# A delta-rule layer's decay gate: softplus as one activation from PSUM, its four activations queued together

## Chip, core and metric

One Trainium2 chip, one of its NeuronCores. The metric is the device time of one launch in microseconds (us). A core has five engines that run their own instruction queues in order: TensorE (PE; its weight loads are shown as PEld), VectorE (DVE), ScalarE (ACT), GpSimd (POOL) and SyncE (SP), which here only starts DMA transfers. Engines wait for each other by semaphores.

## The reference

Six residual steps on x of 1024 tokens by 256 columns: feed-forward, sliding-window attention, feed-forward (twice, with different weights), a gated delta-rule layer with 16 heads of 128, and a last feed-forward. The change is in the delta-rule layer. Cut to what matters:

```python
q = short_conv(hidden @ Wq, conv_q)      # k and v alike: 4 taps, then silu
g = (hidden @ Wfa @ Wfb).reshape(B, T, H, DV) + dt_bias
g = exp(-softplus(g) * exp(A_log))       # the decay gate, per token, head and column
q, k = l2norm(q) * DK ** -0.5, l2norm(k)
def step(S, (qt, kt, vt, gt, bt)):       # over the tokens
    S = S * gt[..., None]
    delta = (vt - einsum("bhk,bhkv->bhv", kt, S)) * bt[..., None]
    S = S + kt[..., None] * delta[:, :, None, :]
    return S, einsum("bhk,bhkv->bhv", qt, S)
```

So for every token, head and column a gate exp(-softplus(z) * a) is computed from z = g + dt_bias, with a one positive number per head.

## The kernel before

**The stages.** Feed-forward and attention take the first 590 us or so; then `delta_rule` runs to the end, with the last feed-forward (`network`) woven into its last turns. The change touches `delta_rule` alone.

**The tiling.** Tokens are cut into 8 tiles of 128, heads into 4 groups of 4. A *pair* is two neighbouring token tiles of one head group; there are 4 x 4 = 16 pairs. Columns of a head lie on the 128 partitions, and a pair's tile is [128, 2 token tiles, 4 heads, 128 tokens], that is 1024 numbers per partition.

**The steps of one pair,** each a Python generator that yields between its steps:

- `prepare`: `convolved` for k and then q. Per head it projects into a PSUM tile `ps` (L641), multiplies the first tap on ScalarE (L653) and adds three taps on VectorE (L655); then Silu over the tile (L660). The squares go to ScalarE (`sq`, L674) and their sums over the partitions to TensorE (`pss`, L678), which VectorE moves out (`ss`, L681). Then the gate: a matmul per head into `pg` (L700), the chain of activations below, and last `pq` (L732), `qk` (L736) and the products `kq` = k times gate on VectorE (L741) and q times gate on POOL (L742).
- `triangle`: seven levels, 1 to 64. Each has matmuls `pm` of k against `kq` (L791; the last is L803), then multiplies `kq` (VectorE, L813) and k (POOL, L819) by the running gate `d`, and puts masked results into `ml` and `qk` (VectorE, L855 and L856). `ml` goes to DRAM as `dm` (L844).
- `solve`: reads blocks of `dm` back (`xb`), scales them into `nb` (L905) and inverts 16 x 16 blocks by small VectorE operations, to `zb` (L943) and on POOL `ztb` (L945); eight transfers (L953, L954) spread them.
- `join`: VectorE steps `four` (L969), `zm` (L972), `four` (L974), `add` (L977), then ScalarE and DMAs to the tiles `z` and `zt`.
- `invert`: matmuls from `pmz` (L1016) on that finish the inverse. `values`, `gates`, `advance` and `emit` make v, the output gate, the recurrent state and the output (`pw`, `pn`, `pso`, `px`).

**The gate's chain before the change** (in `prepare`): per head an Identity from PSUM to SBUF with the bias column dt_bias (L708). Then, over the whole tile, softplus(z) = max(z, 0) + ln(1 + exp(-|z|)): Abs (L716), Exp (L717), Ln (L718) on ScalarE, max and add on VectorE (L720). Last an Exp per head with scale -a (L722) into `ge`. `p["d"]` is `ge`, so the triangle uses it too.

**What sets the order.** The main loop (L1224 on) works on four pairs at once in turn i: `prepare` of pair i+2, `triangle` of pair i+1, `solve`, `join`, `invert`, `values`, `gates` of pair i, and `advance` and `emit` of pair i-1. `weave` sorts the steps: a lane (begin, end, n, steps) has n steps spread evenly between begin and end of the turn; the lane of `prepare` is (0.0, 1.0, 21). On top of that the tile layer schedules: it may move an instruction within its engine's queue by its own estimate of times, so the order of a queue isn't that of the text. `tc.issue_after(ins)` keeps what it encloses behind a given instruction.

**PSUM.** The pool `pj` has three buffers, which `ps`, `pss`, `pg`, `pq`, `ptv`, `pgo` and the last feed-forward's tiles take in turn. An activation function that isn't in ScalarE's loaded table set needs a table load first, an instruction of its own in ScalarE's queue (ACT_TABLE_LOAD in the profile, with the line of the activation that needs it).

Of the kernel before, what the change touches and what calls it, by code (L numbers as in the profile page):

```python
# [1 line left out]

# [8 lines left out]
F32 = mybir.dt.float32  # L11
I32 = mybir.dt.int32
BF16 = mybir.dt.bfloat16
AF = mybir.ActivationFunctionType
ALU = mybir.AluOpType
# [3 lines left out]
P = 128  # L19
# [5 lines left out]
HD = 128  # L25
# [11 lines left out]
HG = 4  # L37
# [441 lines left out]
def key_weights(nc, pool, a, g):  # L479

    cs = slice(g * HG * HD, (g + 1) * HG * HD)
    w = {}
    for nm, src in (("k", "dWk"), ("q", "dWq")):
        w[nm] = pool.tile([P, KC, HG * HD], F32, name=f"w{nm}")
        nc.sync.dma_start(out=w[nm], in_=a[src][:, cs].rearrange("(c p) i -> p c i", p=P))
    w["fb"] = pool.tile([P, HG * HD], F32, name="wfb")
    nc.sync.dma_start(out=w["fb"], in_=a["dWfb"][:, cs])
    return w


def value_weights(nc, pool, a, g):

    cs = slice(g * HG * HD, (g + 1) * HG * HD)
    w = {}
    w["v"] = pool.tile([P, KC, HG * HD], F32, name="wv")
    nc.sync.dma_start(out=w["v"], in_=a["dWv"][:, cs].rearrange("(c p) i -> p c i", p=P))
    w["gb"] = pool.tile([P, HG * HD], F32, name="wgb")
    nc.sync.dma_start(out=w["gb"], in_=a["dWgb"][:, cs])
    w["o"] = pool.tile([P, HG, D], F32, name="wdo")
    nc.sync.dma_start(out=w["o"], in_=a["dWo"][cs, :].rearrange("(h p) d -> p h d", p=P))  # L500
    return w


def delta_rule(tc, a, x, xnT, pp, bc, kon, ones, kdw, first, store, xo):
# [24 lines left out]
    nc = tc.nc  # L529
# [6 lines left out]
    def all_heads(ap):  # L536

        return ap.unsqueeze(1).to_broadcast([P, 2 * HG, ap.shape[1]])

    with ExitStack() as ctx:  # L540
# [3 lines left out]
        pj = ctx.enter_context(tc.tile_pool(name="dpj", reuse_waits="tile", bufs=3, space=PSUM))  # L544
# [12 lines left out]
        faT = cst.tile([P, T], F32, name="faT")  # L557
        gaT = cst.tile([P, T], F32, name="gaT")
        for w, dst in ((wfa, faT), (wga, gaT)):
            for hf in range(2):  # L560
                ps = pj.tile([P, 512], F32, name="ps", tag="pj")
                for c in range(KC):
                    nc.tensor.matmul(
                        ps,
                        lhsT=w[:, c, :],
                        rhs=xnT[:, c, PAD + hf * 512 : PAD + (hf + 1) * 512],
                        start=(c == 0),
                        stop=(c == KC - 1),
# [4 lines left out]
        for n in range(NT):  # L573
            for c in range(KC):
                nc.tensor.matmul(
                    pb[:, n, :],
                    lhsT=xnT[:, c, PAD + n * P : PAD + (n + 1) * P],
                    rhs=wb[:, c, :],
                    start=(c == 0),
                    stop=(c == KC - 1),  # L580
# [3 lines left out]
        nea = cst.tile([P, NH], F32, name="nea")  # L584
# [79 lines left out]
        def prepare(us):  # L664

            g, pr, w = us[0]["g"], us[0]["n"] // 2, us[0]["w"]
            t0 = pr * 2 * P

            ss = small.tile([P, 2, 2, HG], F32, name="ss")
            for i, (nm, ccol) in enumerate((("k", C_CK), ("q", C_CQ))):  # L670
                yield from convolved(us, nm, ccol)
                sq = pre.tile([P, 2, HG, P], F32, name="sq", tag="tmp")
                for c in range(2):
                    nc.scalar.square(sq[:, c], us[0]["p"][nm][:, c])  # L674
                yield
                pss = pj.tile([P, 2, HG], F32, name="pss", tag="pj")
                for c, h, half in parts:
                    nc.tensor.matmul(  # L678
                        pss[half, c, h : h + 1], lhsT=sq[:, c, h, half], rhs=ones, start=True, stop=True
                    )  # L680
                nc.vector.tensor_scalar_add(ss[:, i], pss, 1e-6)  # L681
                yield
            cf = small.tile([P, 2, HG], F32, name="cf", bufs=3)
            nc.vector.reciprocal(cf, ss[:, 0])
            nc.vector.tensor_mul(cf, cf, beta[:, 2 * pr : 2 * pr + 2, g * HG : (g + 1) * HG])
            cfd = us[0]["cfd"] = dram.tile([2, HG, P], F32, name="cfd", bufs=4)
            nc.sync.dma_start(out=cfd.rearrange("c h r -> r c h"), in_=cf)
            kn = small.tile([P, 2, HG], F32, name="kn", bufs=4)
            nc.gpsimd.tensor_tensor(kn, ss[:, 0], plus.rearrange("p (c h) -> p c h", c=2), ALU.pow)

            qe = small.tile([P, 2, HG], F32, name="qe", bufs=5)
            nc.vector.tensor_scalar_mul(qe, ss[:, 1], 1e-6 * HD)


            y = pre.tile([P, 2, HG, P], F32, name="gy", tag="tmp")
            e = pre.tile([P, 2, HG, P], F32, name="ge")
            for h in range(HG):
                if h % 2 == 0:
                    pg = pj.tile([P, 2, 2 * P], F32, name="pg", tag="pj")
                nc.tensor.matmul(  # L700
                    pg[:, h % 2, :],
                    lhsT=w["fb"][:, h * HD : (h + 1) * HD],
                    rhs=faT[:, t0 : t0 + 2 * P],
                    start=True,
                    stop=True,
                )
                hd = C_DTB + g * HG + h
                nc.scalar.activation(  # L708
                    y[:, :, h, :],
                    pg[:, h % 2, :].rearrange("p (c t) -> p c t", t=P),  # L710
                    AF.Identity,
                    bias=pp[:, hd : hd + 1],
                )
                yield
            ef, yf = (t.rearrange("p c h t -> p (c h t)") for t in (e, y))
            nc.scalar.activation(ef, yf, AF.Abs)  # L716
            nc.scalar.activation(ef, ef, AF.Exp, scale=-1.0)  # L717
            nc.scalar.activation(ef, ef, AF.Ln, bias=1.0)  # L718
            yield
            nc.vector.scalar_tensor_tensor(yf, yf, 0.0, ef, ALU.max, ALU.add)  # L720
            for h in range(HG):
                nc.scalar.activation(  # L722
                    e[:, :, h, :], y[:, :, h, :], AF.Exp, scale=nea[:, g * HG + h : g * HG + h + 1]
                )
            yield
            for c, u in enumerate(us):
                u.update(kn=kn[:, c], qe=qe[:, c])
            p = us[0]["p"]
            k, q = p["k"], p["q"]
            pq = pj.tile([P, 2, HG, 64], F32, name="pq", tag="pj")  # L730
            for c, h, half in parts:
                nc.tensor.matmul(  # L732
                    pq[half, c, h], lhsT=k[:, c, h, half], rhs=q[:, c, h, half], start=True, stop=True
                )
            qk = p["qk"] = lev.tile([P, 2 * HG, 64], F32, name="qk", bufs=2)
            nc.vector.tensor_mul(  # L736
                qk, pq.rearrange("p c h t -> p (c h) t"), all_heads(kon[:, K_I : K_I + 64])
            )
            kq = p["kq"] = lev.tile([P, 2, 2, HG, P], F32, name="kq", bufs=3)
            p["d"] = e  # L740
            nc.vector.tensor_mul(kq[:, 0], k, e)  # L741
            nc.gpsimd.tensor_mul(kq[:, 1], q, e)  # L742
            yield
# [474 lines left out]
        for i in range(NG * NT // 2):  # L1218
            g, pr = divmod(i, NT // 2)
            p = dict(turn=turns[i % 2])  # L1220
# [3 lines left out]
        for i in range(-2, len(pairs) + 2):  # L1224
            ahead, mid, now, past = at(i + 2), at(i + 1), at(i), at(i - 1)
            lanes = []
            if ahead:
                g = ahead[0]["g"]
                if g and ahead[0]["n"] == 0:
                    keyw = key_weights(nc, kdw, a, g)  # L1230
                for u in ahead:
                    u["w"].update(keyw)
            if now:
                g = now[0]["g"]
                if g and now[0]["n"] == 0:
                    valw = value_weights(nc, kdw, a, g)
                for u in now:
                    u["w"].update(valw)
            if past:
                lanes.append((0.0, 0.35, 12, chain(advance(past[0]), emit(past[0]), advance(past[1]), emit(past[1]))))  # L1240
            if now:
                lanes.append((0.05, 0.2, 14, solve(now, vbs[i % 2])))
                lanes.append((0.2, 0.35, 6, join(now)))
                lanes.append((0.6, 0.95, 5, invert(now)))
                lanes.append((0.1, 0.65, 7, values(now)))
            if mid:
                lanes.append((0.1, 0.7, 9, triangle(mid)))
            if ahead:
                lanes.append((0.0, 1.0, 21, prepare(ahead)))
            if now:  # L1250
                lanes.append((0.5, 1.0, 2, gates(now)))
            qr = i - len(pairs) + 2
            if qr == 0:
                last_weights()
            if qr >= 0:
                lanes.append((0.2, 0.8, 10, network(qr)))
            weave(*lanes)
# [103 lines left out]
```

## Time and profile before

| | |
|---|---|
| median of three runs | 1770.35 us (1765.06 to 1772.35) |
| span of the profiled execution, first to last instruction | 1763.3 us |
| PE busy | 1409.2 us (80%) |
| VectorE busy | 1236.7 us (70%) |
| ScalarE busy | 847.7 us (48%) |
| POOL busy | 548.2 us (31%) |
| mean granted TensorE clock | 0.886 |
| first and last start of the gate's last Exp (L722) | 645.4 and 1601.7 us |
| ScalarE table loads in the gate | 48 of 1283 ns (L717, L718, L722, 16 each) |
| VectorE step of softplus (L720) | 16 of 1226 ns |
| `kq` on VectorE (L741), one of 16 | 1221 to 3369 ns, median 2252 |

The span is that of one profiled execution; the runs' times come from executions of their own, and the median is 7 us above the span. Busy shares are means over stages with different limits: what a step costs is read from the stage in which it stands, by the engine that waits there and what ends the wait. An operation is named by what it writes and reads ("ge<-gy,nea"), with the line of the kernel.

### The profile page before, as it was taken

The numbers are of one execution on the slowest core, as the hardware profiler recorded it, in microseconds if no ns is written. First come the engines' busy times: TensorE is split into PE (matmuls) and PEld (weight loads), VectorE is DVE, ScalarE is ACT, GpSimd is POOL, SyncE is SP. The second block draws the span as 40 slices with busy tenths as digits, with TensorE's granted clock in tenths as the row PEclk, the third lists the DMA queues.
The fourth block names the chain that finished last, engine by engine and source line by source line (L and its number), as shares of the span: only waits on it lengthen the run. The fifth ranks groups of instructions, "written<-read, shape, count | busy, mean of one in ns | idle before, by whom it ended". The sixth has DMA issues, their size and how long they took to land.

```text
span 1763.3 us, 30888 instructions
## 1 busy us (share of the span) xinstructions
PE 1409.2 (80%) x11697; PEld 1035.2 (59%) x11712; DVE 1236.7 (70%) x2565; ACT 847.7 (48%) x2242; POOL 548.2 (31%) x486
## 2 busy tenths in 40 slices
PE   7986777867899866678867977977887878788996
PEld 3535453635454554466756756765766766676775
DVE  2367889797832247778877787787788688698721
ACT  2227171726222344356646655656645646655431
POOL 0021323231000024244354254353254353354310
PEclk9998898889899967689988888988988988899998
DMA  6020000000200200221121221122221121122100
GB/s 233 1 45 9 5 22 7 5 27 8 89 18 0 48 1 15 35 41 36 34 37 26 46 45 30 32 31 44 41 52 22 35 42 34 34 47 45 30 21 12
DMA packets 185957, 61.09 MB, mean 35 GB/s; under 512 B 148560, under 2 KB 178064, under 8 KB 185552
## 3 DMA queue, kind: packets, MB, share of 16 engines
q1 hardware_dynamic: 185808, 59.11, 15.6%
q8 instruction: 93, 1.52, 0.4%
q14 instruction: 56, 0.46, 0.1%
HBM read 39.64 MB, written 12.75 MB: 30 GB/s over the span
## 4 chain that ended last, share of the span: by engine, by line
PE 34%; DVE 15%; issue 6%; ACT 6%; DMA 5%; POOL 4%; SPq 3%; DVEq 0%; POOLq 0%; ACTq 0%
PE ps L641 4%; PE pm L791 3%; PE po L160 3%; PE pg L135 2%; PE pu L135 2%; DVE k L655 2%; DVE kq L813 2%; PE px L1123 2%; DMA z<-z 2%; PE pss L678 2%; PE pw L1074 1%; PE pgu L1175 1%; PE pgo L762 1%; POOL k L819 1%; DMA dm<-ml 1%
## 5 line engine op out<-in xcount | busy, mean ns | idle before, releaser
L791 PE MATMUL pm<-kq,k 128*64 128x64 f32 x3072 | 140.7, 252 | 133.3 <-DVE kq L741 65.9
L791 PEld LDWEIGHTS pm<-kq,k 128*64 128x64 f32 x3072 | 124.1, 163 | 160.2 <-issue 97.5
L819 POOL TENSOR_TENSOR k<-k,d 128x512 f32<-128x512 f32 x96 | 145.1, 1511 | 197.8 <-PE pm L791 133.8
L813 DVE TENSOR_TENSOR kq<-kq,d 128x1024 f32<-128x1024 f32 x96 | 131.4, 1369 | 56.6 <-PE pm L791 41.5
L323 ACT ACTIVATE e<-ps,nm 128x128 f32<-128x128 f32 x256 | 93.4, 427 | 94.2 <-DVE nm L318 91.4
L641 PE MATMUL ps<-xnT,wv 128*128 128x259 f32 x256 | 86.9, 473 | 25.5 <-DVE k L655 18.6
L655 DVE SCALAR_TENSOR_TENSOR v<-ps,pp,v 128x256 f32<-128x256 f32 x192 | 89.9, 474 | 8.5 <-ACT v L653 7.2
L655 DVE SCALAR_TENSOR_TENSOR q<-ps,pp,q 128x256 f32<-128x256 f32 x192 | 86.2, 475 | 12.7 <-ACT q L653 11.7
L257 PE MATMUL pr<-xnT,wq 128*128 128x512 f32 x128 | 70.0, 678 | 26.9 <-DVE qT L269 11.2
L655 DVE SCALAR_TENSOR_TENSOR k<-ps,pp,k 128x256 f32<-128x256 f32 x192 | 86.0, 473 | 4.5 <-ACT k L653 4.0
L742 POOL TENSOR_TENSOR kq<-q,ge 128x1024 f32<-128x1024 f32 x16 | 45.3, 2831 | 106.3 <-ACT ge L722 95.2
L641 PE MATMUL ps<-xnT,wq 128*128 128x259 f32 x256 | 76.4, 436 | 1.6 <-DVE v L655 1.2
L641 PEld LDWEIGHTS ps<-xnT,wv 128*128 128x128 f32 x256 | 53.6, 229 | 38.4 <-issue 18.5
L369 PE MATMUL po<-wo,oT 128*128 128x256 f32 x256 | 64.2, 395 | 14.7 <-ACT oT L366 10.2
L641 PE MATMUL ps<-xnT,wk 128*128 128x259 f32 x256 | 74.7, 433 | 1.5 <-DVE k L655 1.0
L1123 PE MATMUL px<-wdo,oT 128*128 128x256 f32 x256 | 69.4, 418 | 5.5 <-ACT oT L1119 5.5
L350 POOL TENSOR_TENSOR d<-d,dz 128x512 f32<-128x512 f32 x32 | 35.4, 1108 | 113.5 <-DVE dz L349 58.5
L323 ACT ACTIVATION_READ_ACCUMULATOR e<-ps,nm 128x1 f32 x256 | 66.7, 266 | 0.0
L270 POOL TENSOR_TENSOR qT<-qT,rot 128x512 f32<-128x512 f32 x32 | 43.8, 1367 | 73.1 <-DVE qT L269 55.7
L653 ACT ACTIVATE v<-ps,pp 128x256 f32<-128x256 f32 x64 | 30.0, 470 | 72.5 <-PE ps L641 72.1
L369 PEld LDWEIGHTS po<-wo,oT 128*128 128x128 f32 x256 | 47.8, 194 | 29.1 <-ACT oT L366 15.1
L257 PEld LDWEIGHTS pr<-xnT,wq 128*128 128x128 f32 x128 | 25.0, 210 | 61.6 <-issue 50.1
(236 smaller groups left out, 3860.4 us busy)
## 6 DMA issues: line engine op xcount, KB each, us to landing
zt<-zt SPq DMA_DIRECT2D x32, 256.0 KB, 4.0
dm<-ml SPq DMA_DIRECT2D x64, 64.0 KB, 2.9
z<-z SPq DMA_DIRECT2D x64, 64.0 KB, 4.1
wq<-in_aWq SPq DMA_DIRECT2D x1, 2048.0 KB, 15.0
wo<-in_aWo SPq DMA_DIRECT2D x1, 2048.0 KB
wk<-in_dWk SPq DMA_DIRECT2D x4, 512.0 KB
wq<-in_dWq SPq DMA_DIRECT2D x4, 512.0 KB, 5.0
wv<-in_dWv SPq DMA_DIRECT2D x4, 512.0 KB, 8.5
```

Of the source, the lines that this page charges most:

```text
L135: nc.tensor.matmul(ps[:n], lhsT=w[:, c, cs], rhs=xnT[:, c, cols], start=(c == 0), stop=(c == KC - 1))
L160: nc.tensor.matmul(po, lhsT=hT[:n, ic, i * P : (i + 1) * P], rhs=wd[:n, ic, :], start=(ic == 0), stop=(ic == NI - 1),)
L257: nc.tensor.matmul(pr, lhsT=w[:, c, hcol : hcol + HD], rhs=xnT[:, c, PAD + hf * 512 : PAD + (hf + 1) * 512], start=(c == 0), stop=(c == KC ...
L323: nc.scalar.activation(e[:, s, j, :], ps[:, s, j, :], AF.Exp, bias=nm[:, 4 * s + j : 4 * s + j + 1], scale=SUB**-0.5, accum_out=z[:, s, j ...
L369: nc.tensor.matmul(po, lhsT=oT[:, h, :], rhs=wpool["wo"][:, g * HG + h, :], start=(h == 0), stop=(h == HG - 1),)
L641: nc.tensor.matmul(ps[:, 0 : 2 * P + 3], lhsT=w[nm][:, c, h * HD : (h + 1) * HD], rhs=xnT[:, c, PAD + t0 - 3 : PAD + t0 + 2 * P], start=(c ...
L655: nc.vector.scalar_tensor_tensor(yh, xi, pp[:, col : col + 1], yh, ALU.mult, ALU.add)
L742: nc.gpsimd.tensor_mul(kq[:, 1], q, e)
L791: nc.tensor.matmul(pm[half, :, c * HG + h, :].rearrange("p b (s l) -> p b s l", l=n), lhsT=k[:, c, h, half], rhs=rights(kq[:, :, c, h, half]),
L813: nc.vector.tensor_mul(kqr, kqr, dl.unsqueeze(1).unsqueeze(3).to_broadcast([P, 2, 2 * HG * runs, n]),)
L819: nc.gpsimd.tensor_mul(kl, kl, dr.unsqueeze(2).to_broadcast([P, 2 * HG * runs, n]))
L1123: nc.tensor.matmul(px, lhsT=oT[:, h, :], rhs=u["w"]["o"][:, h, :], start=(h == 0), stop=(h == HG - 1))
```

## The change

Softplus is one ScalarE function. It reads `pg` in PSUM, adds the bias column and writes `gy`; Identity, Abs, Exp, Ln and the VectorE step go. All four projections are made in one step, into two `pg` buffers that both stay in use until the activations have read them. The four Softplus run from the last head to the first, each kept behind the one before; the four Exp are kept behind the last of them. `prepare` has four yields less, and its lane says 17 in place of 21. `gy` and `ge`, and all that follows them, are as before.

```diff
-            for h in range(HG):
-                if h % 2 == 0:
-                    pg = pj.tile([P, 2, 2 * P], F32, name="pg", tag="pj")
-                nc.tensor.matmul(
-                    pg[:, h % 2, :],
-                    lhsT=w["fb"][:, h * HD : (h + 1) * HD],
-                    rhs=faT[:, t0 : t0 + 2 * P],
-                    start=True,
-                    stop=True,
-                )
+            for h2 in range(HG // 2):
+                pg = pj.tile([P, 2, 2, P], F32, name="pg", tag="pj")
+                for h in (2 * h2, 2 * h2 + 1):
+                    nc.tensor.matmul(
+                        pg[:, h % 2].rearrange("p c t -> p (c t)"),
+                        lhsT=w["fb"][:, h * HD : (h + 1) * HD],
+                        rhs=faT[:, t0 : t0 + 2 * P],
+                        start=True,
+                        stop=True,
+                    )
+                pgs = (pgs if h2 else []) + [pg]
+            yield
+            done = None
+            for h in reversed(range(HG)):
                 hd = C_DTB + g * HG + h
-                nc.scalar.activation(
-                    y[:, :, h, :],
-                    pg[:, h % 2, :].rearrange("p (c t) -> p c t", t=P),
-                    AF.Identity,
-                    bias=pp[:, hd : hd + 1],
-                )
-                yield
-            ef, yf = (t.rearrange("p c h t -> p (c h t)") for t in (e, y))
-            nc.scalar.activation(ef, yf, AF.Abs)
-            nc.scalar.activation(ef, ef, AF.Exp, scale=-1.0)
-            nc.scalar.activation(ef, ef, AF.Ln, bias=1.0)
-            yield
-            nc.vector.scalar_tensor_tensor(yf, yf, 0.0, ef, ALU.max, ALU.add)
-            for h in range(HG):
-                nc.scalar.activation(
-                    e[:, :, h, :], y[:, :, h, :], AF.Exp, scale=nea[:, g * HG + h : g * HG + h + 1]
-                )
+                with tc.issue_after(done.ins) if done else nullcontext():
+                    done = nc.scalar.activation(
+                        y[:, :, h, :], pgs[h // 2][:, h % 2], AF.Softplus, bias=pp[:, hd : hd + 1]
+                    )
+            with tc.issue_after(done.ins):
+                for h in range(HG):
+                    nc.scalar.activation(
+                        e[:, :, h, :], y[:, :, h, :], AF.Exp, scale=nea[:, g * HG + h : g * HG + h + 1]
+                    )
             yield
...
-                lanes.append((0.0, 1.0, 21, prepare(ahead)))
+                lanes.append((0.0, 1.0, 17, prepare(ahead)))
```

The lines that follow in the changed kernel stand four lower: L732 there is L736 here, L737 is L741, L787 is L791, L809 is L813, and so on.

More of the change, by code (lines that the diff above doesn't have):

```diff
@@ L1 @@
-from contextlib import ExitStack
+from contextlib import ExitStack, nullcontext
 import ml_dtypes
```

## The prediction

> **What bounds the kernel now.** I read the table of waits first, then the rows by line, then the timeline of one turn of the recurrent loop, then the busy times of its stretches. Only the recurrent stage touches the decay gate: 16 pairs of token tiles, each with one call of `prepare`, one turn of the loop per pair. Of the table of waits these lines bear on the gate (waiting line, what it waited for, us in total, times, longest):
>
> ```profile
> POOL kq L742 <- ACT ge L722: 95.2, 15, 26.4
> PE pm L791 <- DVE kq L741: 65.9, 10, 9.8
> ...
> PE pm L791 <- POOL kq L742: 36.6, 4, 11.4
> ...
> DVE gy L720 <- ACT ge L718: 39.9, 14, 4.2
> ```
>
> TensorE stands still for 65.9 + 36.6 = 102.5 us in 14 places, always in front of the first level of the triangle, until q and k are multiplied by the finished gate. VectorE stands still for 39.9 us until Ln is done. The ScalarE rows of the gate (busy us, mean ns of one):
>
> ```profile
> L708 ACT ACTIVATE gy<-pg,pp 128x256 f32<-128x256 f32 x64 | 27.8, 472 | 33.1 <-PE pg L700 22.6 <-PE pss L678 10.4
> L722 ACT ACTIVATE ge<-gy,nea 128x256 f32<-128x256 f32 x64 | 27.3, 496 | 0.6 <-DVE gy L720 0.4
> L717 ACT ACT_TABLE_LOAD x16 | 20.5, 1283 | 0.3
> L718 ACT ACT_TABLE_LOAD x16 | 20.5, 1283 | 0.3
> L716 ACT ACTIVATE ge<-gy 128x1024 f32<-128x1024 f32 x16 | 16.9, 1057 | 1.4
> L717 ACT ACTIVATE ge<-ge 128x1024 f32<-128x1024 f32 x16 | 16.9, 1057 | 0.2
> ```
>
> How they stand in time, in one turn (start us, us, what, and in brackets idle before and its releaser):
>
> ```profile
> 1269.31 1.06 ACT L716 ACTIVATE ge<-gy 128x1024 f32<-128x1024 f32 x1
> ...
> 1270.86 1.28 ACT L717 ACT_TABLE_LOAD   x1
> 1272.15 1.06 ACT L717 ACTIVATE ge<-ge 128x1024 f32<-128x1024 f32 x1
> 1273.23 1.28 ACT L718 ACT_TABLE_LOAD   x1
> ...
> 1273.96 0.59 SPq L954 DMA_DIRECT2D z<-ztb  x1
> ...
> 1275.61 1.23 DVE L720 SCALAR_TENSOR_TENSOR gy<-gy,ge 128x1024 f32<-128x1024 f32 x1 [4.20 <-ACT ge L718]
> ...
> 1277.62 1.70 ACT L722 ACTIVATE ge<-gy,nea 128x256 f32<-128x256 f32 x4
> ...
> 1278.14 1.89 DVE L969 TENSOR_TENSOR four<-mb,z 128x1024 f32<-128x1024 f32 x1
> ...
> 1280.74 2.58 DVE L741 TENSOR_TENSOR kq<-k,ge 128x1024 f32<-128x1024 f32 x1
> ```
>
> And the busy times of that turn and of its gap (window, length, then PE, PEld, DVE, ACT, POOL busy, granted clock, DMA share, GB/s):
>
> ```profile
> 1220.80:1225.30 4.50, 4.15 (x37) 3.61 (x38) 4.50 (x8) 0.15 (x1) 4.26 (x6) 0.50 0.00 0
> ...
> 1262.00:1275.30 13.30, 12.41 (x129) 10.19 (x126) 7.85 (x22) 10.16 (x15) 0.98 (x1) 1.00 0.21 56
> 1275.30:1283.50 8.20, 0.03 (x2) 0.06 (x3) 7.89 (x9) 6.00 (x18) 5.14 (x3) 0.65 0.17 19
> ```
>
> The reader should see two things. The gate is a serial chain on ScalarE that TensorE waits out. But in that gap VectorE is full (7.89 of 8.20 us): it idled earlier, for Ln, and then works off its queue. So TensorE's 102.5 us can't be taken as the gain; VectorE's order decides.
>
> **The change, per pair, on ScalarE.** Out go four Identity (4 x 0.472 = 1.89), Abs, Exp and Ln over the whole tile (3 x 1.057 = 3.17) and one of three table loads (1.28). In come four Softplus from PSUM. No run here has Softplus; the nearest row is Identity of the same shape, from PSUM with a bias column, 0.472; if it took two passes it would be 0.94 each. I take 0.472, so 1.89. The built order of the changed kernel has two loads per pair (before Softplus, before Exp), so the chain goes from 10.9 to 1.28 + 1.89 + 1.28 + 1.98 = 6.4 us, 4.5 less, and loses its round trip over VectorE (1.23 us of `L720` plus its queue). Where the old chain ran from 1268.4 (second pair of Identity) to 1279.3, the new one needs 5.9 to 6.4, with one 0.6 us copy built in between.
>
> **When the gate is ready.** I count from the end of the Square of q (1261.8 here). Read at the 14 pairs of the steady loop, `ge` now ends 16.3 to 20.5 us after it, mean 18.3. In the changed order Softplus stands straight behind that Square and one or two copies. Its earliest end of the whole chain: `pss` and `pg` on TensorE, 2.2, plus Softplus, load and Exp, 4.9, plus a 0.6 us copy = 7.7. Its latest: if Softplus starts only where the second Identity pair starts now (7.4 on the mean), 7.4 + 6.4 = 13.8. VectorE gets to the `kq` multiply, once `qk` is done, 11.0 us after the Square on the mean. I take the gate as ready before that, at about 9. Multiply and POOL's half (2.35 to 2.84 in this timeline) then end near 11.5 to 13; the first triangle matmul starts 22 after the Square now (mean).
>
> **What the turn gains.** The mean turn is 64.4 us (770.3 to 1607.5 in 13 turns). In the built order `kq` now comes before `four`, the first step of `join`, so I follow VectorE's loop: `four` to the first triangle multiply L813, to the masks of level 16, over DRAM to `nb`, the solve to `zb`, the DMAs of z, `four` again.
> - `four` to L813: mean 9.8 now, as `kq`, `L974` and often `L977` stand between. After: `four` 1.2 to 1.9, `zm` 1.21, two conv steps 0.95, `om` 0.14 = 3.5 to 4.2; I take 4.3. That is -5.5.
> - `ztb` to `four`: mean 7.7 now. The last z transfer is issued at 1273.96 and needs about 1.9 to land (median of its row), 1275.9, and `four` starts at 1278.14; at the 14 pairs it could start 1.7 earlier on the mean and no more. -1.7.
> - Solve: the built order puts five conv steps of q (0.40 to 0.47 each) between its small operations: 0 to +2.4; I take +2.4, since `nb` itself waits for DMA, not for them.
> - Triangle: `L974` and `L977` (about 1.3 each) move behind L813: 0 to +2.6. VectorE is busy 30.6 of 36.7 us there, so half hides: +1.3.
>
> The sum is -3.5 per turn, x 14 = -49 us. The two pairs before the loop fills have nothing to hide the chain (TensorE waits 9.4 and 11.4 us there): 4.5 + 1.23 each, -11. The sum of the bounds per turn runs from -5.5 - 1.7 = -7.2 to -5.5 - 1.7 + 2.4 + 2.6 = -2.2.
>
> **Costed at nothing, and what is new behind what.** `prepare` is spread over 17 instead of 21 steps, so the last q projection is issued later: only some 6.3 us of matmuls stand between it and `pss`, where about 10 stood, and the way from it over conv steps, Silu and Square is 10.4 us (1251.4 to 1261.8). That puts a new TensorE wait of about 4 us in front of `pss`; it lies inside the time that TensorE now gains, and without that cover it would cost 4 x 14 = 56. On VectorE the `kq` multiply now waits for `ge` itself; three conv steps of k, the state update and `four` are queued behind it, so each us by which `ge` comes later than 11.0 costs one. Both `pg` buffers stay held to the last Softplus, and `pq` needs one of them: `pq` starts 7.7 after the Square now, Softplus ends near 5 to 6, so nothing. No DMA is added or removed. POOL keeps its work.
>
> **The skill against the rows.** "ScalarE: Activation LUTs", section "Table sets: the hidden batching unit", says Exp and Ln share a set and need one load. Here L717, L718 and L722 each load, 16 times: three per pair. By the page the old chain would hold one load and the change would add one, a gain of 1.9 instead of 4.5 per pair; the rows decide. Section "What ACT_TABLE_LOAD costs" gives about 2.66 us per switch with its drain; here Exp starts 0.01 us after a load of 1.28. By the page the removed load would be worth 22 us more in all.
>
> **Rivals.**
> (B) TensorE's wait goes entirely, 102.5 us: 1770 - 102 = 1668. For it: clock 0.50 after the gap against 1.00 before, so shorter gaps also speed the matmuls behind them. Against it: VectorE, 51 us busy of the 64.4, full in the gap.
> (C) The join sets the turn: only the 1.7 us at `four` is won, x 14 = 24, so 1746; with the solve's +2.4 nothing, 1770. For it: turns with almost no wait at `pm` (0.1 us before 1480.8) are no shorter than the others (67.3).
> (D) Slower: `pq` is held up by the two buffers. From `pq` to `pm` TensorE has some 7.5 us of work (`pq` 1.15, k projections 3.1, `pn`, `pso`, v projections 1 each), and `pm` starts 22 us after the Square now; so from a Softplus end of 14.5 on, each us costs 14. At 17.5: 1770 + 42 = 1812. For it: the wait on `pg` and `pss` (33 us idle at L708), and copies that wait for the inversion ahead of Softplus. Against it: Identity ends 8.2 after the Square on the mean, 10.9 at most.
> (E) The change splits its queue, a load per activation: the built order shows one load per four, so I give it no chance of its own.
>
> **Numbers.** The profiled execution has a span of 1763.3; its own time is not listed, and the median of the three runs, 1770.35, is 7 above the span, which the forecast keeps. 1770 - 49 - 11 = 1710. Chances: this case 0.45 (1690 to 1733: the bounds of the turn but for their ends), B 0.25, C 0.20, D 0.10. 0.5% is 9 us, about what can be told from no change. Faster: 0.45 + 0.25 + 0.15 of C = 0.85; same: 0.05 of C and 0.01 of D; slower 0.09. The range goes from the low bound, 7.2 x 14 + 11 = 112 less, 1658, to the middle of C, 1750.
>
> **What would show it.** After: two table loads in the gate per pair, Softplus near 0.47 us; VectorE's 39.9 us wait gone; `pm` L787 waits for `kq` L737 far less than 102 us; new waits of `pss` for the Square and of the second triangle level for L809; `four` waiting for its DMA; turns of about 61. A Softplus of 0.9 us, a `pq` that waits for ScalarE, or turns still at 64 would prove me wrong.

## The result, and the profile after

| | before | after |
|---|---|---|
| median of four runs each | 1771.35 us | 1793.61 us (1793.32 to 1793.83) |
| ratio | 1 | 1.0131, 95% interval 1.0091 to 1.0171 |
| span of the profiled execution | 1763.3 us | 1791.8 us |
| mean granted TensorE clock | 0.886 | 0.875 |

The kernel became 1.3% slower. The forecast was 1710 us, and 1793.61 lies outside its range as well.

The page of the changed kernel, its span and the first part (busy us, share of the span, instructions):

```profile
span 1791.8 us, 30807 instructions
...
PE 1444.0 (81%) x11697; PEld 1051.3 (59%) x11712; DVE 1197.4 (67%) x2549; ACT 780.0 (44%) x2178; POOL 573.8 (32%) x486
```

VectorE lost 39 us of work and ScalarE 68, and the kernel is longer. ScalarE's 68 are about what the diff takes out; of VectorE's 39 the diff takes out 20 (L720, 16 of 1.23 us), and 13 come from `kq`, which took 2199 ns on the mean before and takes 1362 now. The rows of the gate in the changed kernel (busy us, mean ns of one, then idle before):

```profile
L718 ACT ACTIVATE ge<-gy,nea 128x256 f32<-128x256 f32 x64 | 28.7, 500 | 0.2
L713 ACT ACTIVATE gy<-pg,pp 128x256 f32<-128x256 f32 x64 | 25.1, 475 | 0.2
...
L713 ACT ACT_TABLE_LOAD x16 | 20.5, 1283 | 45.5 <-PE pg L700 31.6 <-PE pss L678 13.9
L718 ACT ACT_TABLE_LOAD x16 | 20.5, 1283 | 0.3
```

Softplus takes 475 ns, and two loads per pair remain of three. So the new chain is as short as forecast. Its table of waits (us in total, times, longest):

```profile
PE pm L787 <- POOL k L815: 76.7, 29, 4.2
...
DVE nb L901 <- DMA xb<-dm: 63.1, 15, 12.1
...
DVE kq L737 <- ACT ge L718: 33.4, 15, 3.0
...
PE pss L678 <- ACT sq L674: 18.9, 6, 8.0
...
PE pm L787 <- POOL kq L738: 4.5, 4, 3.1
```

The waits for the gate's products in front of the triangle, 102.5 us before, are down to 4.5 on POOL's half, and none is listed on VectorE's. Two others have grown: TensorE now waits 76.7 us for POOL's multiply of k (11.1 before), and VectorE 63.1 us for the transfer that brings the blocks of `dm` back. The two stood in the table of waits of the kernel before as

```profile
DVE nb L905 <- DMA xb<-dm: 17.5, 11, 3.9
...
PE pm L791 <- POOL k L819: 11.1, 9, 2.3
```

To see what a turn gained and lost I cut it at instructions that every kernel has, and took means over the 14 turns from the second pair on, in us. "DMA way" runs from the first issue of `dm` to the start of `nb`; the triangle runs from the first multiply L813 (L809 after) to the last mask of level 16, with the 0.2 us or less to the issue.

| | `four` to triangle | triangle | DMA way | `nb` to `zb` | `zb` to `four` | turn |
|---|---|---|---|---|---|---|
| before | 9.8 | 27.3 | 9.7 | 10.1 | 8.2 | 65.2 |
| after | 4.2 | 28.3 | 13.9 | 12.5 | 7.9 | 66.8 |

Without the DMA way a turn is 2.6 us shorter; the DMA way is 4.2 longer. In the span: 21.9 over the 14 turns, 0.9 ahead of them and 5.6 behind, together 28.4 of 1791.8 - 1763.3 = 28.5.

What lengthens the DMA way is seen in the timeline. First a turn of the kernel before, then one of the changed one (start us, us, what, idle before and its releaser):

```profile
1243.24 0.36 SPq L687 DMA_DIRECT2D cfd<-cf  x1
...
1251.04 2.59 SPq L844 DMA_DIRECT2D dm<-ml  x4
...
1257.44 0.59 SPq L888 DMA_DIRECT2D xb<-dm  x1
```

```profile
1258.27 0.36 SPq L687 DMA_DIRECT2D cfd<-cf  x1
1260.23 2.59 SPq L840 DMA_DIRECT2D dm<-ml  x4
...
1266.96 0.93 PE L799 MATMUL pm<-kq,k 128*64 128x128 f32 x5 [1.44 <-issue]
...
1267.48 0.47 ACT L653 ACTIVATE q<-ps,pp 128x256 f32<-128x256 f32 x1 [2.19 <-remote]
...
1269.97 1.14 PE L799 MATMUL pm<-kq,k 128*64 128x128 f32 x8 [2.08 <-issue]
...
1272.54 0.59 SPq L884 DMA_DIRECT2D xb<-dm  x1
1275.40 0.42 DVE L901 SCALAR_TENSOR_TENSOR nb<-xb,diag 64x256 f32<-64x256 f32 x1 [3.03 <-DMA xb<-dm]
```

`xb` may be issued only when `dm` has landed. That took 1257.44 - 1253.63 = 3.8 us from the last issue of `dm` in the one, and 1272.54 - 1262.82 = 9.7 us in the other. Ahead of `dm` stands a small transfer that the diff doesn't touch: L687 writes `cf`, 8 coefficients per partition, to DRAM as `cfd`, transposed, so that each of its 1024 words of 4 bytes is a piece of its own. Before, it was issued 5 to 18 us ahead of `dm`; now it stands 1.8 to 2.0 us ahead in nine of fifteen pairs, some 5 in two, and behind the first `dm` transfer in four. The DMA issues of the kernel before (KB each, median us from issue to landing) say how long such a write is under way:

```profile
dm<-ml SPq DMA_DIRECT2D x64, 64.0 KB, 2.9
xb<-dm SPq DMA_DIRECT2D x16, 64.0 KB, 2.7
...
cfd<-cf SPq DMA_DIRECT2D x16, 4.0 KB, 10.7
```

4 KB take 10.7 us where 64 KB take 2.9. (The trace shows only two landings of this write, 9.1 and 12.3 us, and 10.7 is the middle of them.) So a write that was over, or nearly over, when `dm` was issued now runs beside it. That is a theory (T1): the write of `cfd` holds up transfers that are issued while it is under way, and the change moved it beside `dm`. The pairs of the kernel before already differ in this way: in the seven with the write 11 us or more ahead of `dm`, `xb` is issued 1.6 to 1.8 us behind the last `dm` transfer; in the eight with 10 us or less it is 1.7 to 5.9. The rival, T2, is that the write does no harm there and the time comes from elsewhere in the change, such as the new order or the lane.

### The profile page after: what moved, and what is told of

It is laid out like the page before. It is cut to its first block, busy times and chain, and to the rows that moved or that the text cites. A ratio compares the mean times of both kernels' runs of the same rounds, so it can differ in the third digit from the quotient of the medians.

```text
span 1791.8 us, 30807 instructions
## 1 busy us (share of the span) xinstructions
PE 1444.0 (81%) x11697; PEld 1051.3 (59%) x11712; DVE 1197.4 (67%) x2549; ACT 780.0 (44%) x2178; POOL 573.8 (32%) x486
## 4 chain that ended last, share of the span: by engine, by line
PE 37%; POOL 12%; DVE 8%; ACT 6%; DMA 5%; issue 5%; SPq 1%; another core or an unknown queue 0%; POOLq 0%; DVEq 0%; ACTq 0%
PE ps L641 5%; POOL d L817 4%; PE pm L787 3%; PE px L1119 3%; POOL k L815 3%; PE po L160 3%; PE pu L135 2%; PE pg L135 2%; DMA xb<-dm 2%; POOL kq L738 2%; PE pss L678 2%; DVE kq L809 2%; PE pg L700 2%; PE pgu L1171 2%; DMA dm<-ml 1%
## 5 line engine op out<-in xcount | busy, mean ns | idle before, releaser
L815 POOL TENSOR_TENSOR k<-k,d 128x512 f32<-128x512 f32 x96 | 154.7, 1612 | 243.0 <-PE pm L787 161.8
L787 PE MATMUL pm<-kq,k 128*64 128x64 f32 x3072 | 137.8, 248 | 93.0 <-POOL k L815 76.7
L787 PEld LDWEIGHTS pm<-kq,k 128*64 128x64 f32 x3072 | 120.8, 159 | 124.3 <-POOL k L815 91.7
L809 DVE TENSOR_TENSOR kq<-kq,d 128x1024 f32<-128x1024 f32 x96 | 128.0, 1334 | 55.1 <-PE pm L799 19.7
L655 DVE SCALAR_TENSOR_TENSOR q<-ps,pp,q 128x256 f32<-128x256 f32 x192 | 86.1, 474 | 13.9 <-ACT q L653 13.1
L257 PE MATMUL pr<-xnT,wq 128*128 128x512 f32 x128 | 69.9, 676 | 26.7 <-DVE nm L318 11.2
L641 PE MATMUL ps<-xnT,wk 128*128 128x259 f32 x256 | 84.4, 466 | 7.1 <-DVE k L655 6.5
L641 PE MATMUL ps<-xnT,wq 128*128 128x259 f32 x256 | 83.0, 465 | 8.0 <-DVE q L655 8.0
L653 ACT ACTIVATE k<-ps,pp 128x256 f32<-128x256 f32 x64 | 29.9, 470 | 118.4 <-PE ps L641 118.2
L1119 PE MATMUL px<-wdo,oT 128*128 128x256 f32 x256 | 76.8, 452 | 5.0 <-ACT oT L1115 5.0
L641 PE MATMUL ps<-xnT,wv 128*128 128x259 f32 x256 | 77.4, 431 | 2.6 <-DVE k L655 2.3
L941 POOL TENSOR_TENSOR ztb<-vb,diag 64x256 f32<-64x256 f32 x16 | 15.3, 956 | 199.8 <-DVE vb L936 121.9
L738 POOL TENSOR_TENSOR kq<-q,ge 128x1024 f32<-128x1024 f32 x16 | 53.3, 3334 | 79.7 <-ACT ge L718 79.7
L350 POOL TENSOR_TENSOR d<-d,dz 128x512 f32<-128x512 f32 x32 | 35.3, 1104 | 112.9 <-DVE dz L349 62.4
L817 POOL TENSOR_TENSOR d<-d 128x256 f32<-128x256 f32 (+2 forms) x96 | 67.5, 703 | 3.4
L1119 PEld LDWEIGHTS px<-wdo,oT 128*128 128x128 f32 x256 | 57.1, 232 | 17.1 <-ACT oT L1115 7.3
L323 ACT ACTIVATION_READ_ACCUMULATOR e<-ps,nm 128x1 f32 x256 | 66.8, 267 | 0.0
```

What stands on the lines that cost most here:

```text
L257: nc.tensor.matmul(pr, lhsT=w[:, c, hcol : hcol + HD], rhs=xnT[:, c, PAD + hf * 512 : PAD + (hf + 1) * 512], start=(c == 0), stop=(c == KC ...
L323: nc.scalar.activation(e[:, s, j, :], ps[:, s, j, :], AF.Exp, bias=nm[:, 4 * s + j : 4 * s + j + 1], scale=SUB**-0.5, accum_out=z[:, s, j ...
L641: nc.tensor.matmul(ps[:, 0 : 2 * P + 3], lhsT=w[nm][:, c, h * HD : (h + 1) * HD], rhs=xnT[:, c, PAD + t0 - 3 : PAD + t0 + 2 * P], start=(c ...
L655: nc.vector.scalar_tensor_tensor(yh, xi, pp[:, col : col + 1], yh, ALU.mult, ALU.add)
L787: nc.tensor.matmul(pm[half, :, c * HG + h, :].rearrange("p b (s l) -> p b s l", l=n), lhsT=k[:, c, h, half], rhs=rights(kq[:, :, c, h, half]),
L809: nc.vector.tensor_mul(kqr, kqr, dl.unsqueeze(1).unsqueeze(3).to_broadcast([P, 2, 2 * HG * runs, n]),)
```

## The experiments

**Other pieces, same place.** Two edits, each put into both kernels, change only the pieces in which `cf` is written (and how `diag` reads them, in the second). In the traces VectorE, ScalarE, POOL and SyncE run the same instructions in the same order as without the edit. In the *wide* form it goes out as 128 pieces of 32 bytes, which puts the coefficients in another order, so the blocks are scaled by the wrong ones:

```diff
-            nc.sync.dma_start(out=cfd.rearrange("c h r -> r c h"), in_=cf)
+            nc.sync.dma_start(out=cfd.rearrange("c h r -> (c h r)").rearrange("(p e) -> p e", e=2 * HG), in_=cf.rearrange("p c h -> p (c h)"))
```

In the *read* form it is stored as it lies, 32 bytes per partition, and `diag` picks its words out as it reads:

```diff
-            cfd = us[0]["cfd"] = dram.tile([2, HG, P], F32, name="cfd", bufs=4)
-            nc.sync.dma_start(out=cfd.rearrange("c h r -> r c h"), in_=cf)
+            cfd = us[0]["cfd"] = dram.tile([P, 2, HG], F32, name="cfd", bufs=4)
+            nc.sync.dma_start(out=cfd, in_=cf)
...
-            nc.sync.dma_start(out=diag, in_=us[0]["cfd"].rearrange("c h (b i) -> (c h b) i", i=BLK))
+            nc.sync.dma_start(out=diag, in_=bass.AP(tensor=us[0]["cfd"].tensor, offset=us[0]["cfd"].offset, ap=[[1, 2 * HG], [2 * HG * BLK, P // BLK], [2 * HG, BLK]]))
```

The changed kernel, wide:

> The changed kernel, but the transfer of the 1024 coefficients cf to DRAM writes 128 runs of 32 bytes instead of 1024 words of 4 bytes; they then lie in another order, so the solve gets other coefficients. All five queues keep their order. Theory 1 (the 4-byte writes, now started 2 us before the transfers of dm instead of 8 to 14, hold those up): VectorE's wait of nb for xb falls from 63 us to under 20, the xb load follows the last dm start by about 2 us at every pair instead of 5 to 11, and the time falls by 6 us at 13 pairs, to about 1715. Theory 2 (the new order of VectorE and POOL in the triangle sets the turn, the DMA wait only fills slack): within 10 us of 1794.

The kernel before, wide:

> The same edit in the kernel before (other coefficients in the solve, same order of all queues). There cfd starts 5 to 18 us ahead of dm, and the xb load follows dm by 1.6 to 5.9 us. Theory 1: a small gain, the excess over 1.7 us, some 1.2 us at 14 pairs, so 1755 (at most 1740). Theory 2: no change, 1770.

The changed kernel, read:

> The changed kernel with the coefficients stored as they lie (128 runs of 32 bytes) and put in order when they are read back (1024 reads of 4 bytes, a turn later). Theory 1, if 4-byte reads don't hold up others as 4-byte writes do: like the run that writes in wide runs, about 1715. If reads are as bad, the diag load, which is issued behind the z transfers, delays something there: 1740 to 1800. Theory 2: 1794.

The kernel before, read:

> The kernel before with cf stored as it lies in SBUF (32 bytes per partition) and diag read back word by word, the same results as before. T1: as with the wide write, 1729 within 8 us (0.970 of before), and the step from here to the changed kernel with the same edit (1692) is what softplus is worth by itself, about 37 us. T2 (4-byte reads hold up xb as 4-byte writes held up dm): the gain is lost, 1760 to 1780.

| | median us | ratio to before, 95% | `four` to triangle | triangle | DMA way | `nb` to `zb` | `zb` to `four` | turn |
|---|---|---|---|---|---|---|---|---|
| before, wide | 1728.84 | 0.9696 (0.9635 to 0.9758) | 9.9 | 26.7 | 8.0 | 9.8 | 8.1 | 62.6 |
| before, read | 1728.47 | 0.9716 (0.9680 to 0.9752) | 9.9 | 26.5 | 8.0 | 9.8 | 8.2 | 62.4 |
| after, wide | 1691.69 | 0.9496 (0.9432 to 0.9559) | 4.2 | 28.2 | 7.7 | 11.9 | 7.8 | 59.9 |
| after, read | 1691.97 | 0.9496 (0.9436 to 0.9556) | 4.4 | 28.3 | 7.8 | 11.9 | 7.9 | 60.3 |

T1 holds, and by more than I had expected: 102 us in the changed kernel (1793.61 to 1691.97; the kernel before had medians from 1771 to 1780 beside these runs), and 50 in the kernel before (1778.88 beside its read form to 1728.47), whose DMA way of 9.7 us was lengthened too. (Of the 2.8 us per turn that the kernel before loses, 1.7 are in the DMA way and 0.8 in the triangle.) The mean granted TensorE clock differs as well, 0.875 in the changed kernel and 0.900 in its read form; but 6.1 of the 6.5 us between their turns lie in the DMA way, where VectorE waits for transfers. The DMA issues of the kernel before in its wide form:

```profile
dm<-ml SPq DMA_DIRECT2D x64, 64.0 KB, 2.2
xb<-dm SPq DMA_DIRECT2D x16, 64.0 KB, 2.7
...
cfd<-cf SPq DMA_DIRECT2D x16, 4.0 KB, 1.5
```

The same 4 KB land in 1.5 us instead of 10.7, and `dm` in 2.2 instead of 2.9. The long wait for `xb` in the table of waits of the changed kernel, read form, has gone:

```profile
PE pm L787 <- POOL k L815: 75.5, 28, 4.2
...
DVE kq L737 <- ACT ge L718: 35.8, 16, 3.0
...
DVE nb L901 <- DMA xb<-dm: 9.8, 9, 4.1
```

The read form of the changed kernel, 1691.97 us, is faster than both kernels. Against the read form of the kernel before it also says what the change is worth where the write does no harm: 1728.47 - 1691.97 = 36.5 us. By the two ratios that is 0.9496 / 0.9716 = 0.977, with both intervals 0.970 to 0.985.

**The same write, elsewhere.** The changed kernel keeps its 1024 words, but `cfd` is issued behind the last `mb` load of the next turn (the first pair's at once):

```diff
+        late = []
+
+        def put_cf(behind):
+
+            with tc.issue_after(behind.ins):
+                while late:
+                    cfd, cf = late.pop(0)
+                    nc.sync.dma_start(out=cfd.rearrange("c h r -> r c h"), in_=cf)
...
-            nc.sync.dma_start(out=cfd.rearrange("c h r -> r c h"), in_=cf)
+            late.append((cfd, cf))
...
+            if any(c is us[0]["cfd"] for c, _ in late):
+                cfd, cf = late.pop(0)
+                nc.sync.dma_start(out=cfd.rearrange("c h r -> r c h"), in_=cf)
...
-                nc.sync.dma_start(out=mb[32 * j : 32 * j + 32], in_=mb[0:32])
+                got = nc.sync.dma_start(out=mb[32 * j : 32 * j + 32], in_=mb[0:32])
+            put_cf(got)
```

> The changed kernel with its write of cfd exactly as it is (1024 words of 4 bytes per pair), but put behind the mb loads of the next turn in SP's queue, so that neither dm nor xb stands beside it. T1 (the write costs only what it holds up, and next to dm it holds up dm and xb): from dm's last issue to xb's falls from 6.4 to about 2 us, the turn from 66.8 to about 60.5, the time to 1695 to 1715; the z transfers follow some 10 us behind and may lose a little. T2 (a write of 4-byte words costs the same wherever it stands, since it takes the DMA engines): the time stays at 1780 to 1800.

Measured 1699.67 us, 0.9558 (0.9531 to 0.9584), turn 61.0, and 1.8 us from the last issue of `dm` to that of `xb`, as T1 had it; VectorE, ScalarE and POOL keep the order of the changed kernel. The mirror takes the kernel before and ties the write behind the last `dm` transfer:

```diff
-            nc.sync.dma_start(out=cfd.rearrange("c h r -> r c h"), in_=cf)
+            with tc.issue_after(put[0].ins) if put else nullcontext():
+                nc.sync.dma_start(out=cfd.rearrange("c h r -> r c h"), in_=cf)
...
-                            nc.sync.dma_start(
+                            put[0] = nc.sync.dma_start(
```

> The mirror: the kernel before, softplus as it was, with the write of cfd put straight behind the four dm transfers and ahead of xb in SP's queue (before, it is issued 5 to 18 us ahead of dm). Nothing else changes. T1: xb or nb now waits for the end of that write, about 7 us more than the 3.6 of the kernel before where the whole write is in front of xb, less what VectorE has to do meanwhile: 4 to 7 us x 14 turns = 56 to 98, so 1830 to 1875. T2 (the place does not matter): 1765 to 1785, as before.

Measured 1867.99 us, 1.0508 (1.0459 to 1.0558). So the one write, shifted by some microseconds in its queue, moves the old kernel up by 89 us and the new one down by 94. "Nothing else changes" doesn't quite hold here: the scheduler also gave some 470 of VectorE's 2565 instructions another place in its queue. The next two runs have this same order and other pieces, so they tell the two apart; and of the 9.1 us that a turn is longer than in the read form of the kernel before, the DMA way has 8.7. The mirror's DMA issues and, below, one wait of its table:

```profile
dm<-ml SPq DMA_DIRECT2D x64, 64.0 KB, 2.2
...
xb<-dm SPq DMA_DIRECT2D x16, 64.0 KB, 11.5
...
cfd<-cf SPq DMA_DIRECT2D x16, 4.0 KB, 12.4
```

```profile
DVE nb L908 <- DMA xb<-dm: 142.6, 16, 11.6
```

`dm`, issued ahead of the write, lands in 2.2 us as without it. `xb`, issued some 1.6 us behind it, lands in 11.5, at about the end of it. (These are few landings, two of `xb` and one of `cfd`; the wait of `nb` has all 16.) Being ahead is no full protection, though: in the changed kernel the write was issued right behind the last `dm` transfer in four pairs, and in one of them `xb` followed only 10.9 us later, in the others 1.6 to 1.7.

**What in it does the harm.** In the mirror's place, first 512 pieces of 8 bytes, then 256 of 16. Here `cfd` is shaped [4, P, 2] or [2, P, 4], and `diag` is read back by words, in 4 or 2 transfers instead of one:

```diff
-                nc.sync.dma_start(out=cfd.rearrange("c h r -> r c h"), in_=cf)
+                nc.sync.dma_start(out=cfd.rearrange("g r e -> r g e"), in_=cf.rearrange("p c h -> p (c h)").rearrange("p (g e) -> p g e", e=2))
```

> The kernel before with the write of cfd straight behind the dm transfers, as in the mirror (1868 us), but cfd laid out so that it is written as 512 pieces of 8 bytes in place of 1024 of 4; diag is read back word by word, which cost nothing in another run (1728). T1 (each small piece costs alike, the bytes do not matter): half of the mirror's 140 us over 1728, so 1785 to 1810; nb waits about 7.5 us behind xb's issue where it was 11.6 and 3.1. T2 (only words of 4 bytes are hit): 1728 to 1745. T3 (a small write costs the same whatever its pieces): 1855 to 1880.

> The same with 256 pieces of 16 bytes. T1: a quarter of the 140 us, 1755 to 1775, nb some 5 us behind xb's issue. T2: 1728 to 1745. T3: 1855 to 1880.

Then the read of `diag` in that place, 1024 words of 4 bytes again, in the read form of the kernel before (the line is cut short here, and `put[0]` is the last `dm` transfer as in the mirror):

```diff
-            nc.sync.dma_start(out=diag, in_=bass.AP(
+            with tc.issue_after(put[0].ins):
+                nc.sync.dma_start(out=diag, in_=bass.AP(
```

> The kernel before with cf stored as it lies, and the read of diag, 1024 words of 4 bytes from DRAM, put straight behind the dm transfers and ahead of xb, in the very place where the write stood in the mirror. T1 (a read of 4-byte words holds nothing up): 1728 to 1745; nb waits for diag and xb together, 3 to 4 us behind xb's issue. T2 (reads hold up what follows as writes do, and were harmless only for their place): about as the mirror, 1840 to 1875.

| behind `dm` | median us | over the read form, 1728.47 | ratio to before, 95% | `xb` issued to `nb`, us |
|---|---|---|---|---|
| 1024 writes of 4 bytes | 1867.99 | 139.5 | 1.0508 (1.0459 to 1.0558) | 11.6 |
| 512 writes of 8 bytes | 1747.79 | 19.3 | 0.9851 (0.9799 to 0.9903) | 5.1 |
| 256 writes of 16 bytes | 1731.35 | 2.9 | 0.9748 (0.9710 to 0.9786) | 3.7 |
| 1024 reads of 4 bytes | 1728.72 | 0.3 | 0.9722 (0.9674 to 0.9770) | 3.3 |

The 16-byte write came out as T2 said, the 8-byte write 3 us above T2's range: the price is not one per piece (T1; 8 bytes would have cost 70) nor one per transfer (T3), and not quite one of 4-byte words alone. The wait behind `xb`'s issue, less the 3.1 us it has anyhow, is 8.5, 2.0 and 0.6 us. The three writes have the same order of VectorE, ScalarE and POOL, so their differences are those of the pieces and of the 1, 4 or 2 transfers that read them back. The reads cost nothing; 0.3 and also 2.9 us are inside the spread of the runs. In the timeline of that run the transfers follow each other as ever:

```profile
1222.86 2.59 SPq L846 DMA_DIRECT2D dm<-ml  x4
1225.50 0.62 SPq L888 DMA_DIRECT2D diag<-cfd  x1
1228.49 0.62 SPq L891 DMA_DIRECT2D xb<-dm  x1
```

The Trainium skill, "DMA: Bandwidth & Descriptors", section "Specifications", says that below 512 bytes an SDMA engine reads, modifies and writes. That fits writes being hurt where reads are not. But its bound doesn't tell where harm begins here: pieces of 32 bytes landed in 1.5 us, and pieces of 16 cost 2.9 us in all. Smaller pieces also mean that pieces of more partitions lie side by side in the same stretch of DRAM, as the write is transposed; size and neighbourhood were not separated. Which part of the chip does the holding up, no run here shows.

**The lane.** The diff also sets `prepare`'s lane from 21 to 17. Back at 21 in the changed kernel, and then in its read form:

```diff
-                lanes.append((0.0, 1.0, 17, prepare(ahead)))
+                lanes.append((0.0, 1.0, 21, prepare(ahead)))
```

> The changed kernel with the lane of prepare back at 21: its 17 steps then end at 0.8 of the turn. Theory 1 in its wider form (the lane of 17 makes the sums of squares of k, and with them cfd, come later against dm): cfd starts 6 us or more ahead of dm again and the time falls to 1770 or below. If the lane is not what moved cfd: the gap stays near 2 us and the time near 1794.

> The changed kernel with cf stored as it lies and the lane of prepare back at 21 instead of 17. T1 (the lane did harm only by where it put the write of cfd): as with lane 17, 1692 within 8 us; from first triangle multiply to the next about 60. T2 (the lane matters of itself, since the last q projection comes late and TensorE waits for the Square before pss, 18.9 us in all against 10.7): some 10 to 20 us faster than lane 17, 1672 to 1682. T3 (21 steps where the generator has 17 leave the last ones bunched, and kq comes early or late in a bad way): slower, 1700 to 1730.

Measured: 1772.64 us, 0.9962 (0.9930 to 0.9993), a little above T1's 1770, where `cfd` is issued 4 to 12 us ahead of `dm` and the DMA way is 11.0 us; and 1714.00 us, 0.9624 (0.9592 to 0.9656), in the read form. The lane of 17 costs 21 us with the harmful write (1793.61 against 1772.64, or 30 by the two ratios to the kernel before) and gains 22 without it. The lane moves much else in all queues, so the two runs give sums and not the price of `cfd`'s place alone. The second result is what T3 said; why 21 is worse there I did not follow beyond its longer way from `four` to the triangle, 6.6 us instead of 4.4.

**Half of the change alone.** Read form, Softplus kept, but without the rule that queues the four Softplus and four Exp together:

```diff
-                with tc.issue_after(done.ins) if done else nullcontext():
+                with nullcontext():
...
-            with tc.issue_after(done.ins):
+            with nullcontext():
```

> The changed kernel with cf stored as it lies (1692 us), without the rule that queues the four Softplus and the four Exp together: the scheduler then splits some of them two and two, which makes 16 more table loads in all, 16 x 1.283 = 20.5 us of ScalarE. This takes back the second half of the change and keeps the first. T1 (ScalarE is not what the turn waits for, the gate is ready before VectorE comes to it): 1685 to 1702. T2 (the gate is still what kq waits for, so the loads and the longer chain fall on the turn): 1705 to 1725.

Measured 1708.63 us, 0.9610 (0.9581 to 0.9638): T2. Against the read form, 1691.97, the order is worth about 17 of the 36.5 us. Rows by line and a wait of this run:

```profile
L713 ACT ACT_TABLE_LOAD x24 | 30.8, 1283 | 37.2 <-PE pss L678 30.6 <-PE pg L700 6.4
L718 ACT ACT_TABLE_LOAD x24 | 30.8, 1283 | 0.4
```

```profile
DVE kq L737 <- ACT ge L718: 68.1, 16, 7.2
```

48 loads instead of 32, and VectorE waits 68.1 us for the gate instead of 35.8. So the gate's chain still sets when `kq` can start.

## Why the prediction was wrong

The step that failed is the sentence "No DMA is added or removed" among the edits costed at nothing. It was true, and it was the wrong question: a DMA was moved. The lane of 17 makes the sums of squares of k, and so `cf` and the issue of `cfd`, come later against `dm`. Of the lane I only said that "the last q projection is issued later" and priced it in front of `pss`. The row of 10.7 us for 4 KB stood in the list of DMA issues that I had read, and the issue of `cfd` 7.8 us ahead of `dm` in the timeline; together they say that in such a turn the write hadn't landed when `dm` was issued. I did not set them side by side, and none of my rivals was this. In place of the nothing that I put down, the runs showed 4.2 us more of DMA way per turn, and a changed kernel that is 94 us faster with the same write issued elsewhere and 102 us faster with the write whole.

Point by point, by the read forms of both kernels, where the write is harmless:

- Softplus at 0.472 us each, two loads per pair: right, 475 ns and 32 loads.
- The gate ready at about 9 us after the Square of q: 10.4 on the mean of the 14 pairs (9.1 to 12.5). That it would be ready before VectorE comes to `kq` was wrong: `kq` waits for it in all 16 pairs, 35.8 us, and a longer chain falls on the turn: 61.3 us instead of 60.3 in the run without the rule.
- `four` to the triangle, -5.5: right, 9.9 to 4.4.
- Solve, +2.4: right, 9.8 to 11.9. The triangle, +1.3: it is 1.8, from 26.5 to 28.3. "POOL keeps its work" was too simple: its multiply of k became slower, 1448 ns to 1649, and TensorE waits 75.5 us for it instead of 11.0. Why it is slower was not tried. So TensorE's wait did go from in front of the first level, as rival B had it, but most of it came back at another place.
- `ztb` to `four`, -1.7: wrong, 8.2 to 7.9. I read 1.7 us of slack in front of `four` from when its last transfer could have landed; with `kq` out of the way less than 0.4 came back.
- The sum per turn, -3.5: -2.1, from 62.4 to 60.3, so -29 and not -49 over 14 turns.
- The pairs before the loop fills, -11: -4.9 (first multiply of the second pair at 700.0 and 695.1 us).
- Not foreseen: the end behind the last pair's first multiply, +8.6 us (149.2 to 157.8). It is no new wait for the most part: that multiply now stands earlier among the other work. TensorE is busy 131.07 us in that stretch of the kernel before, 136.86 in that of the changed one, with 1007 weight loads instead of 984.
- `pq` not held up by the two `pg` buffers (rival D): right, `pq` waits 4.4 us for Softplus in all of the changed kernel's profile. The new wait of TensorE for the Square before `pss`, about 4 us a turn, hardly came: 18.9 us in 6 places there, 10.7 in 3 before, and 10.8 and 10.1 us in all in the read forms.

So -29 - 5 + 9 = -25 between the two profiled executions of the read forms (1722.9 and 1697.7), and -36.5 between their medians; the other 11 us are the choice of execution, since the profiled ones took 1699.52 us, 8 above their median, and 1724.69 us, 4 below theirs. The direction of the reasons was right, and their sum of 60 us too large, against 25 to 36.5; but the sign of the result was set by the write. The read form's 1692 us lies near the forecast of 1710 partly by luck, since it starts from a kernel before of 1728 and not of 1770.

Small slips of the working change none of this: the chain's earliest end takes 4.9 us for Softplus, load and Exp, whose own terms give 5.15; the upper bound of the turn, -2.2, gives 1728 and not 1733; the middle of C's 1746 to 1770 is 1758 and not 1750.

## What to carry to other kernels

When a change moves a step, list the transfers that the step issues and what stands next to each in its queue before and after, and set the time each takes to land against the time to its next neighbour. A row of DMA issues in which 4 KB land later than 64 KB is a cost that waits for its place: here it took 50 us from the old kernel and 102 from the new one. A transposing write of single words to DRAM is better turned round, so that the write is whole and the read picks the words.

## What the runs showed of the hardware

1024 writes of 4 bytes to DRAM held up a 64 KB read, issued 1.6 us behind them in the turns looked at, until 11.5 us after its issue, and in the same place 1024 reads of 4 bytes held up nothing. The price fell faster than the number of pieces: 8.5, 2.0 and 0.6 us for 1024, 512 and 256 pieces of the same 4 KB.

The DMA engines need not be busy for it. Of the changed kernel, busy times of the stretch from `cfd` to `xb` (length, then PE, PEld, DVE, ACT, POOL, granted clock, DMA share, GB/s):

```profile
1258.20:1272.50 14.30, 10.39 (x145) 8.14 (x142) 9.08 (x16) 8.15 (x27) 7.88 (x6) 0.86 0.51 20
```

and of the mirror from `cfd` to the start of `nb`:

```profile
1231.80:1244.60 12.80, 11.73 (x81) 9.39 (x82) 2.91 (x6) 8.76 (x18) 1.05 (x1) 0.73 0.14 13
```

At 20 GB/s the engines show a share of 0.51 beside `dm`, but 0.14 in the mirror, where the wait is as long. The traces' records of single DMA packets say more. The write's own 1024 packets are over 1.5 to 3.8 us behind its issue in all pairs of both kernels and of the mirror, though it lands 9.1 to 12.4 us behind it; what is slow is what comes after them. In the turn of the kernel before, the 1536 packets of 64 bytes of `xb` and the load behind it run within 1.3 us; in the mirror they spread over 10.4. In the changed kernel's turn single packets of `dm` last up to 2.0 us, in that of the kernel before at most 0.06.

Fetches of instructions are held up too. A packet of 16 KB from the queue that the page calls "instruction" takes 1.0 to 1.2 us (median) in the delta-rule stage of every run. The longest took 4.1 to 5.7 us in each of the five runs that write 1024 words of 4 bytes, and at most 1.8 us in each of the nine others.

TensorE and ScalarE stop as well, as the turn above shows, for 1.44, 2.08 and 2.19 us: at `issue`, where the profile shows nothing that they waited for, and at `remote`, another core or a queue it doesn't know. In the read form of the changed kernel the waits at `remote` in this stage are gone. That the engines waited for instructions would explain it, but isn't shown: in the turn above no fetch is recorded between 1258.42 and 1269.94 us.
